# Bilinear field pairs: weight loads in ring order, four-field loads split into single ones, more splits dealt out

## The chip, the cores and the metric

The kernel runs on one core of a Trainium2 chip. The metric is the device time of one execution in microseconds; the time of a kernel is the median of its runs. Five engines share the work: TensorE (PE, with its weight loads as PEld), VectorE (DVE), ScalarE (ACT), GpSimd (POOL) and SyncE (SP), which here only issues transfers. ACT and POOL issue transfers too.

## The reference

There are 32 fields of 128 numbers for each of 1024 rows, and a 128x128 matrix for each of the 496 pairs of fields (i, j) with i < j. Field i goes through the pair's matrix, and the result is multiplied by field j, element by element:

```
v_i = inputs[:, I_IDX, :]
v_j = inputs[:, J_IDX, :]
transformed = jnp.einsum('bpd,ped->bpe', v_i, W)
return transformed * v_j
```

All is float32. The output is 1024 x 496 x 128 numbers, 260 MB, so the stores are by far the largest traffic.

## The kernel before, in words

**Tiling.** Fields lie as 128 x 1024 tiles (embedding on the partitions, rows along the free axis). Pairs are numbered q = 0 to 495 in the order of line 45: i falls from 30 to 0, and j runs upward from i+1. So field i becomes the left operand at q = first_q[i] = (30-i)(31-i)/2, for 31-i pairs. The host lays the weights out as 62 tiles of eight pairs (512 KB each).

**Arithmetic.** The first 15 pairs use plain float32 products (line 227). For the other 481, both operands are split into a high part h and a low part l, and a third part d made from them (names wh, wl, wd and xh, xl, xd). A pair then takes three products for each half of 512 columns: xh·wh and xl·wl (line 230), a scaling of the sum by ACT in place (line 232), and xd·wd added to it (line 241). VectorE multiplies the whole pair, 1024 columns, by field j into an output tile (line 251). An output tile holds four pairs; ACT issues its 2 MB store (line 280).

**Splits.** `split_w` handles two pairs' weights, called a chunk: ACT makes wh (line 137), POOL makes wl and wd (lines 139 to 141). `split_x` handles half a field: ACT makes xh (line 155), POOL makes xl (lines 156 and 157), and VectorE makes xd (line 290) ten half-pair steps later (XDLAG). The list `todo` gives each split the earliest pair at which it may be put into the program. At most one split is taken per pair, the one needed first. A chunk for pair q may be split from pair q-5 on. A field may be split from the start of the field before it, plus one pair (line 174). For fields 1 to 11 (SPREAD = 12, lines 175 and 176) the two halves are dealt out: they come n/5 and 3n/5 pairs after that, where n = 30-i.

**Loads.** SP issues most loads, in program order, and waits at each until its buffer is free. Weight tiles rotate through a ring of three buffers; field 0 (`load_x(0)`) takes one of them once. Weight tiles 12, 14, ... 60 (WAPART) are loaded in two parts, 112 partitions by POOL and 16 by SP (lines 105 and 106), and are put into the program as soon as the tile three places before has been split (lines 286 and 287). The other weight tiles and field 0 have pair numbers worked out ahead (lines 191 to 197): tile c at pair 8c-17, or 8c-11 for tiles 55 and 57; field 0 at 421. Fields 16 to 1 come in four groups of four, each one 2 MB transfer (`load_group`, line 111) at the pairs 52, 141, 219 and 313. For this the host interleaves the four fields of a group, so that a partition's 16 KB lie together.

**Buffers.** There are three output tiles, and each of the four groups' buffers is a further output tile until 20 pairs before its load (`until`, OWAIT). So output tiles fall from seven to three in the course of the run. Four PSUM tiles hold a pair each.

Of the kernel before, what the change touches and what calls it, by code (L numbers as in the profile page):

```python
# [7 lines left out]
F32 = mybir.dt.float32  # L8
# [3 lines left out]
P = 128  # L12
NF = 32
NQ = NF * (NF - 1) // 2
BT = 1024
HB = 512
WC = 2
WL = 8
# [3 lines left out]
SHARED = 26  # L22
XDLAG = 10
LAG = 3
SPREAD = 12
PB = 4
WB = 3
WLEAD = 12
XAFTER = 54
XLEAD = 5  # L30

XG = 4
NE = 14
ROWS = 8 * NE
WAPART = tuple(range(12, 62, 2))
BACK = 3
XAT = (313, 219, 141, 52)
OWAIT = 20
SLAG = 2
PB = 4  # L40

# [7 lines left out]
def kernel(  # L49
# [22 lines left out]
    nc = tc.nc  # L72
# [3 lines left out]
    xpool = ctx.enter_context(tc.tile_pool(name="x", bufs=1))  # L76
# [6 lines left out]
    x_sb = {}  # L83

    def load_x(f, pieces=1, eng=None):
        if f == 0:

            t = rpool.tile([P, WL, P], F32, tag="w", name="x_0").rearrange("p q e -> p (q e)")
        else:
            t = xpool.tile([P, BT], F32, tag=f"x{f}", name=f"x_{f}")  # L90
        s = BT // pieces
        for k in range(pieces):
            (eng or nc.sync).dma_start(out=t[:, k * s : (k + 1) * s], in_=xt[f, :, k * s : (k + 1) * s])  # L93
        x_sb[f] = t

    w_raw = {}
# [3 lines left out]
    def move_on(k):  # L100

        nc.gpsimd.dma_start(out=mark[: 2 * k], in_=xt[0, : 2 * k, :16].rearrange("(b a) n -> a b n", a=k))  # L102

    def load_apart(dst, src):
        nc.gpsimd.dma_start(out=dst[:ROWS], in_=src[:ROWS].rearrange("(b a) m n -> a b m n", a=NE))
        nc.sync.dma_start(out=dst[ROWS:], in_=src[ROWS:])

    def load_group(k):
        t = xpool.tile([P, XG, BT], F32, tag=f"g{k}", name=f"x_g{k}")
        f = XG * k + 1  # L110
        nc.sync.dma_start(out=t, in_=xt[f : f + XG].rearrange("m d b -> (m d b)").rearrange("(d m b) -> d m b", m=XG, b=BT))
        for m in range(XG):
            x_sb[f + m] = t[:, m, :]

    def load_w(c, splits=(0, WL), eng=nc.sync):
        w_raw[c] = rpool.tile([P, WL, P], F32, tag="w", name=f"w_{c}")
        if c in WAPART:
            load_apart(w_raw[c], wt[c])
            return
        for a, b in zip(splits, splits[1:]):  # L120
            eng.dma_start(out=w_raw[c][:, a:b, :], in_=wt[c, :, a:b, :])
# [8 lines left out]
    w_s, spent = {}, []  # L130
# [18 lines left out]
    def split_x(f, a, u):  # L149

        if a == 0:
            x_s[f] = [spool.tile([P, BT], F32R, tag=t, name=f"{t}_{f}") for t in ("xh", "xl", "xd")]
        s = slice(a, a + HB)
        h, l, d = [t[:, s] for t in x_s[f]]
        nc.scalar.mul(h, x_sb[f][:, s], 1.0 - 2.0**-13)  # L155
        nc.gpsimd.tensor_tensor(l, x_sb[f][:, s], h.bitcast(F32), ALU.subtract)  # L156
        nc.gpsimd.tensor_scalar(l, l.bitcast(F32), 1.0 / EPS, 1.0, ALU.mult, ALU.mult)  # L157
        if f > NF - 2 - NATIVE - SHARED:
            later.append((min(u + XDLAG, 2 * first_q[f] + LAG - 1), d, h.bitcast(F32), l.bitcast(F32)))
        else:  # L160
            nc.gpsimd.tensor_tensor(d, h.bitcast(F32), l.bitcast(F32), ALU.subtract)
# [3 lines left out]
    first_q = {i: q for q, (i, j) in reversed(list(enumerate(pairs)))}  # L165
# [6 lines left out]
    for i in range(NF - 2 - NATIVE, -1, -1):  # L172
        for a in range(0, BT, HB):
            at = first_q[i + 1] + 1 if i < NF - 3 - NATIVE else 2
            if 0 < i < SPREAD:
                at += (NF - 2 - i) * (1 + 2 * (a > 0)) // 5
            todo.append((at, first_q[i], lambda u, i=i, a=a: split_x(i, a, u)))
    todo.sort(key=lambda t: t[1])

# [5 lines left out]
    load_w(1, eng=nc.sync)  # L185
    for f in range(NF - 5, NF - 4 - XLEAD, -1):
        load_x(f)
# [3 lines left out]
    w_at = {}  # L191
    for c in range(WB, -(-NQ // WL)):
        free = (c - WB + 1) * WL if (c - WB) * WL < nq0 else 0
        early = 0 if XAFTER < c <= XAFTER + WB else WLEAD - 6
        if c not in WAPART:
            w_at[max(c * WL - 3 * WC - 5 - early, free)] = c
    x_at = XAFTER * WL - 11
    assert x_at not in w_at and len(w_at) == NQ // WL - WB - len(WAPART)

    back = []  # L200
    w_next = list(WAPART)

    ngroup = NF // XG // 2
    group_at = {q: k for k, q in enumerate(XAT)}
    assert all(q < first_q[XG * k + XG + 1] for q, k in group_at.items())
    until = {f"g{k}": q - OWAIT for q, k in group_at.items()}
    used = {t: n - 9 for n, t in enumerate(("s0", "s1", "s2", *sorted(until, reverse=True)))}

    def out_tile(g):
# [9 lines left out]
    def first(u):  # L219
        q, h = divmod(u, 2)  # L220
        i, c = pairs[q][0], q // WC
        r = slice(q % WC * P, (q % WC + 1) * P)
        s = slice(h * HB, (h + 1) * HB)
        if h == 0:
            po[q] = ppool.tile([P, BT], F32, tag="po", name=f"po_{q}")
        if q < nq0:
            nc.tensor.matmul(po[q][:, s], w_raw[q // WL][:, q % WL, :], x_sb[i][:, s], start=True, stop=True)  # L227
        else:
            for t in (0, 1):
                m = nc.tensor.matmul(po[q][:, s], w_s[c][t][:, r], x_s[i][t][:, s], start=t == 0, stop=t == 1)  # L230
                apart(m, scaled.get(u - 1) if h else None)
            scaled[u] = nc.scalar.mul(po[q][:, s], po[q][:, s], 1.0 + EPS)  # L232
            apart(scaled[u], taken.get(q - PB), "TensorE's products, which this waits for, have waited for it")

    def second(u):
        q, h = divmod(u, 2)
        i, j = pairs[q]
        r = slice(q % WC * P, (q % WC + 1) * P)
        s = slice(h * HB, (h + 1) * HB)
        if q >= nq0:  # L240
            m = nc.tensor.matmul(  # L241
                po[q][:, s], w_s[q // WC][2][:, r], x_s[i][2][:, s], start=False, stop=True, skip_group_check=True
            )
            apart(m, scaled[u ^ 1])
        g, k = divmod(q, OG)
        if k == 0 and h == 0:
            ots[g] = out_tile(g)
        if q >= NQ - 2:
            nc.vector.tensor_tensor(ots[g][:, k, s], po[q][:, s], x_sb[j][:, s], ALU.mult)  # L249
        elif h == 1:  # L250
            taken[q] = nc.vector.tensor_tensor(ots[g][:, k, :], po.pop(q), x_sb[j], ALU.mult)  # L251
        if q >= NQ - 2:
            stores.append((u + SLAG, out[g, :, k, s], ots[g][:, k, s]))
        elif g == 0 or q >= NQ - OG:
            if h == 1:
                stores.append((u + SLAG, out[g, :, k], ots[g][:, k]))
        elif k == OG - 1 and h == 1:
            stores.append((u + SLAG, out[g], ots[g]))

    for u in range(2 * NQ + LAG + SLAG):  # L260
        q = u // 2
        if u < 2 * NQ:
            i, j = pairs[q]
            if u % 2 == 0 and j == i + 1 and XG * ngroup < i - 2 - XLEAD:
                load_x(i - 2 - XLEAD)
            first(u)
            if u == 2 * nq0:
                move_on(5)
            if u % 2 == 0 and q in group_at:
                load_group(group_at[q])  # L270
            if u % 2 == 1 and q in w_at:
                load_w(w_at[q])
            if u % 2 == 0 and q in back:
                move_on(16 - NE if w_next else 13)
            if u == 2 * x_at + 1:
                load_x(0)
        if LAG <= u < 2 * NQ + LAG:
            second(u - LAG)
        while stores and stores[0][0] <= u - LAG:
            nc.scalar.dma_start(*stores.pop(0)[1:])  # L280
        if u % 2 == 1:
            ready = [t for t in todo if t[0] <= q]
            if ready:
                ready[0][2](u)
                todo.remove(ready[0])
        if w_next and (XAFTER if w_next[0] == XAFTER + 2 else w_next[0] - WB) in spent:
            load_w(w_next.pop(0))
            back.append(q + BACK)
        while later and later[0][0] <= u:
            nc.vector.tensor_tensor(*later.pop(0)[1:], ALU.subtract)  # L290
    assert not todo and not later and not stores
# [32 lines left out]
```

## Time and profile before

| What | us |
|---|---|
| median of three runs (745.08, 750.95, 749.3) | 749.3 |
| the profiled execution | 751.61 |
| its span, first to last instruction | 749.8 |
| PE busy in the span | 706.0 |
| DVE busy | 641.1 |
| ACT busy | 634.3 |
| POOL busy | 596.2 |

The mean granted clock of TensorE is 0.982. HBM traffic is 49.29 MB read and 260.05 MB written. The span is the time in which instructions ran; the profiled execution's own time is 1.8 us longer. PE busy is no measure of PE at its peak, since the matmuls overlap. A row of the profile's groups gives line, engine, operation, tile written from tile read, shape, count, busy time, mean duration in ns, and then the engine's idle time just before such instructions with what ended it.

### The profile page before, as it was taken

The page shows a single profiled execution, that of the slowest core. Times are in us where ns is not written, and L with a number is a line of the kernel's source. Part 1 is how long each engine was busy: PE and PEld are TensorE (multiplying, and loading weights), DVE is VectorE, ACT ScalarE, POOL GpSimd, SP SyncE. Part 2 cuts the span into 40 slices and gives each one's busy share as a digit, 9 for nine tenths or more (in the row PEclk, how much of TensorE's full clock was granted, in tenths as well). Part 3 has the DMA queues.
Part 4 walks back from the last instruction along what each step waited for, and adds up shares of the span by engine and source line. Part 5 has one row for each costly group of instructions (what it writes and reads, how often), then busy time and mean ns, then how long its engine had stood idle before and what let it go on. Part 6 is the DMA issues. An engine that isn't in the chain of part 4 may idle for free.

```text
span 749.8 us, 10632 instructions
## 1 busy us (share of the span) xinstructions
PE 706.0 (94%) x2946; PEld 554.3 (74%) x2946; DVE 641.1 (85%) x550; ACT 634.3 (85%) x1256; POOL 596.2 (80%) x882
## 2 busy tenths in 40 slices
PE   7999999989999999997999979799999999999894
PEld 3577777777787788885888858688787778777783
DVE  3888999979999999996999959688998888988785
ACT  1298999979999999996999959699899999988893
POOL 1789999988888988986888867768788878887660
PEclk9999999999999999999999989999999999999997
DMA  9999999999999999999999999999999999999988
GB/s 346 421 432 425 427 428 429 423 409 377 407 423 414 422 425 426 424 426 418 426 424 425 424 426 378 420 425 422 412 424 418 420 423 415 409 406 412 422 365 340
DMA packets 32939, 310.04 MB, mean 413 GB/s; under 512 B 5104, under 2 KB 5232, under 8 KB 16752
## 3 DMA queue, kind: packets, MB, share of 16 engines
q10 hardware_dynamic: 19584, 261.10, 83.0%
q1 hardware_dynamic: 8864, 36.77, 12.3%
q0 software_dynamic: 4432, 11.48, 4.1%
q8 instruction: 24, 0.39, 0.2%
q14 instruction: 35, 0.29, 0.1%
HBM read 49.29 MB, written 260.05 MB: 413 GB/s over the span
## 4 chain that ended last, share of the span: by engine, by line
PE 64%; DMA 18%; DVE 10%; issue 3%; ACT 3%; ACTq 0%; POOL 0%; DVEq 0%
PE po L230 40%; PE po L241 20%; DMA out_dram<-ot 17%; DVE ot L251 7%; PE po L227 4%; DVE xd L290 3%; ACT po L232 2%; DMA x<-in_xt_dram 1%; ACT wh L137 0%; DVE ot L249 0%; ACTq L280 0%; POOL wl L139 0%; ACT xh L155 0%; DVEq L251 0%; ACTq L93 0%
## 5 line engine op out<-in xcount | busy, mean ns | idle before, releaser
L232 ACT ACTIVATE po<-po 128x512 f32<-128x512 f32 x962 | 553.1, 584 | 82.7 <-PE po L230 66.4
L251 DVE TENSOR_TENSOR ot<-po,x 128x1024 f32<-128x1024 f32 x358 | 430.8, 1221 | 75.6 <-DMA out_dram<-ot 25.6
L230 PE MATMUL po<-xh,wh 128*128 128x512 f32 x962 | 383.0, 398 | 24.0 <-DVE ot L251 23.0
L241 PE MATMUL po<-xd,wd 128*128 128x512 f32 x962 | 377.9, 393 | 4.8 <-DVE ot L249 2.4
L230 PE MATMUL po<-xl,wl 128*128 128x512 f32 x962 | 378.2, 393 | 3.2 <-POOL wl L139 3.0
L139 POOL TENSOR_TENSOR wl<-w,wh 128x256 fp32r<-128x256 f32 x241 | 186.2, 773 | 74.9 <-ACT wh L137 69.3
L230 PEld LDWEIGHTS po<-xh,wh 128*128 128x128 f32 x962 | 182.2, 189 | 79.6 <-DVE ot L251 42.0
L241 PEld LDWEIGHTS po<-xd,wd 128*128 128x128 f32 x962 | 182.3, 190 | 45.5 <-DVE ot L249 3.2
L230 PEld LDWEIGHTS po<-xl,wl 128*128 128x128 f32 x962 | 182.3, 190 | 41.3 <-POOL wl L139 4.1
L141 POOL TENSOR_TENSOR wd<-wl,wd 128x256 fp32r<-128x256 f32 x241 | 181.1, 751 | 20.1
L251 DVE TENSOR_TENSOR ot<-po,x_g 128x1024 f32<-128x1024 f32 x136 | 165.0, 1223 | 24.2 <-DMA out_dram<-ot 6.7
L140 POOL TENSOR_SCALAR wd<-wh 128x256 fp32r<-128x256 f32 x241 | 100.4, 417 | 20.5
L137 ACT ACTIVATE wh<-w 128x256 fp32r<-128x256 f32 x241 | 98.6, 410 | 7.9 <-DVE ot L251 3.6
L290 DVE TENSOR_TENSOR xd<-xh,xl 128x512 fp32r<-128x512 f32 x52 | 50.6, 974 | 0.3 <-ACT wh L137 0.3
L156 POOL TENSOR_TENSOR xl<-x_g,xh 128x512 fp32r<-128x512 f32 x32 | 41.7, 1304 | 0.5
L157 POOL TENSOR_SCALAR xl<-xl 128x512 fp32r<-128x512 f32 x52 | 36.0, 692 | 4.7
L156 POOL TENSOR_TENSOR xl<-x,xh 128x512 fp32r<-128x512 f32 x20 | 26.3, 1315 | 15.7 <-ACT xh L155 15.5
L227 PE MATMUL po<-x,w 128*128 128x512 f32 x60 | 29.3, 646 | 4.0 <-DMA x<-in_xt_dram 3.9
L227 PEld LDWEIGHTS po<-x,w 128*128 128x128 f32 x60 | 11.9, 205 | 20.6 <-issue 14.4
L155 ACT ACTIVATE xh<-x 128x512 fp32r<-128x512 f32 x20 | 12.3, 624 | 11.4 <-DMA x<-in_xt_dram 11.3
L155 ACT ACTIVATE xh<-x_g 128x512 fp32r<-128x512 f32 x32 | 20.0, 625 | 0.0
L102 POOL DMA_DIRECT2D mark<-in_xt_dram x26 | 16.6, 637 | 0.0
(7 smaller groups left out, 19.9 us busy)
## 6 DMA issues: line engine op xcount, KB each, us to landing
out_dram<-ot ACTq DMA_DIRECT2D x122, 2048.0 KB, 12.6
w<-in_wt_dram SPq DMA_DIRECT2D x36, 512.0 KB, 10.9
w<-in_wt_dram POOLq DMA_DIRECT2D x25, 448.0 KB, 11.6
x_g<-in_xt_dram SPq DMA_DIRECT2D x4, 2048.0 KB, 18.6
x<-in_xt_dram SPq DMA_DIRECT2D x14, 512.0 KB, 9.6
out_dram<-ot ACTq DMA_DIRECT2D x6, 512.0 KB, 8.3
w<-in_wt_dram SPq DMA_DIRECT2D x26, 64.0 KB, 6.4
x<-in_xt_dram ACTq DMA_DIRECT2D x4, 256.0 KB, 5.8
```

The lines of the kernel that those rows point to most:

```text
L137: halved[c] = nc.scalar.mul(h, raw, 1.0 - 2.0**-13)
L139: nc.gpsimd.tensor_tensor(l, raw, h.bitcast(F32), ALU.subtract)
L140: nc.gpsimd.tensor_scalar(d, h.bitcast(F32), EPS, 1.0, ALU.mult, ALU.mult)
L141: nc.gpsimd.tensor_tensor(d, l.bitcast(F32), d.bitcast(F32), ALU.subtract)
L156: nc.gpsimd.tensor_tensor(l, x_sb[f][:, s], h.bitcast(F32), ALU.subtract)
L157: nc.gpsimd.tensor_scalar(l, l.bitcast(F32), 1.0 / EPS, 1.0, ALU.mult, ALU.mult)
L227: nc.tensor.matmul(po[q][:, s], w_raw[q // WL][:, q % WL, :], x_sb[i][:, s], start=True, stop=True)
L230: m = nc.tensor.matmul(po[q][:, s], w_s[c][t][:, r], x_s[i][t][:, s], start=t == 0, stop=t == 1)
L232: scaled[u] = nc.scalar.mul(po[q][:, s], po[q][:, s], 1.0 + EPS)
L241: m = nc.tensor.matmul(po[q][:, s], w_s[q // WC][2][:, r], x_s[i][2][:, s], start=False, stop=True, skip_group_check=True)
L251: taken[q] = nc.vector.tensor_tensor(ots[g][:, k, :], po.pop(q), x_sb[j], ALU.mult)
L290: nc.vector.tensor_tensor(*later.pop(0)[1:], ALU.subtract)
```

## The change: what it does

1. Weight tiles from 12 on, and field 0 among them, are put into the program in one order, `ring`: each as soon as the ring's buffer it takes has been split. For odd tiles this is pair 8c-23 in place of 8c-17. Field 0 stands between tiles 54 and 55, and the tile that takes its buffer is now 57; before it was 58, which stood ahead of 57.
2. A group's four fields are loaded by four transfers of 512 KB each, the highest field first, at the group's pair and 6, 12 and 18 pairs later (XSTEP). They still fill one buffer. The host's interleaving goes.
3. SPREAD goes from 12 to 18, so fields 12 to 17 are dealt out too. The second half now comes 5n/10 pairs after the start in place of 6n/10, for all dealt fields; the first half is as it was.

VectorE's whole-pair multiplication (line 251 before) stands in both kernels alike. The core of the diff:

```
-SPREAD = 12
+SPREAD = 18
+WRING = 12
+XSTEP = 6
...
-    def load_group(k):
-        t = xpool.tile([P, XG, BT], F32, tag=f"g{k}", name=f"x_g{k}")
-        f = XG * k + 1
-        nc.sync.dma_start(out=t, in_=xt[f : f + XG].rearrange("m d b -> (m d b)").rearrange("(d m b) -> d m b", m=XG, b=BT))
-        for m in range(XG):
-            x_sb[f + m] = t[:, m, :]
+    group = {}
+
+    def load_group(k, m):
+        if m == XG - 1:
+            group[k] = xpool.tile([P, XG, BT], F32, tag=f"g{k}", name=f"x_g{k}")
+        f = XG * k + 1 + m
+        x_sb[f] = group[k][:, m, :]
+        nc.sync.dma_start(out=x_sb[f], in_=xt[f])
...
+        if f == 0 and a > 0:
+            spent.append("x")
...
-                at += (NF - 2 - i) * (1 + 2 * (a > 0)) // 5
+                at += (NF - 2 - i) * (2 + 3 * (a > 0)) // 10
...
-        early = 0 if XAFTER < c <= XAFTER + WB else WLEAD - 6
-        if c not in WAPART:
-            w_at[max(c * WL - 3 * WC - 5 - early, free)] = c
-    x_at = XAFTER * WL - 11
+        if c < WRING:
+            w_at[max(c * WL - 3 * WC + 1 - WLEAD, free)] = c
...
-    w_next = list(WAPART)
+    last = NQ // WL
+    ring = [*range(WRING - WB, XAFTER + 1), "x", *range(XAFTER + 1, last)]
...
-    group_at = {q: k for k, q in enumerate(XAT)}
+    group_at = {q + XSTEP * (XG - 1 - m): (k, m) for k, q in enumerate(XAT) for m in range(XG)}
...
-                move_on(16 - NE if w_next else 13)
-            if u == 2 * x_at + 1:
-                load_x(0)
+                move_on(16 - NE if max(w_raw) < WAPART[-1] else 13)
...
-        if w_next and (XAFTER if w_next[0] == XAFTER + 2 else w_next[0] - WB) in spent:
-            load_w(w_next.pop(0))
-            back.append(q + BACK)
+        if ring[WB:] and ring[0] in spent:
+            ring.pop(0)
+            c = ring[WB - 1]
+            if c == "x":
+                load_x(0)
+            else:
+                load_w(c)
+            if c in WAPART:
+                back.append(q + BACK)
...
-    for f in range(1, XG * 4, XG):
-        xt[f : f + XG] = xt[f : f + XG].transpose(1, 0, 2).copy().reshape(XG, P, BT)
```

More of the change, by code (lines that the diff above doesn't have):

```diff
@@ L193 @@
         free = (c - WB + 1) * WL if (c - WB) * WL < nq0 else 0
-        early = 0 if XAFTER < c <= XAFTER + WB else WLEAD - 6
-        if c not in WAPART:
-            w_at[max(c * WL - 3 * WC - 5 - early, free)] = c
-    x_at = XAFTER * WL - 11
-    assert x_at not in w_at and len(w_at) == NQ // WL - WB - len(WAPART)
+        if c < WRING:
+            w_at[max(c * WL - 3 * WC + 1 - WLEAD, free)] = c
     back = []
-    w_next = list(WAPART)
+    last = NQ // WL
+    ring = [*range(WRING - WB, XAFTER + 1), "x", *range(XAFTER + 1, last)]
     ngroup = NF // XG // 2
-    group_at = {q: k for k, q in enumerate(XAT)}
-    assert all(q < first_q[XG * k + XG + 1] for q, k in group_at.items())
-    until = {f"g{k}": q - OWAIT for q, k in group_at.items()}
+    group_at = {q + XSTEP * (XG - 1 - m): (k, m) for k, q in enumerate(XAT) for m in range(XG)}
+    assert all(q + 5 < first_q[XG * k + m + 2] for q, (k, m) in group_at.items())
+    until = {f"g{k}": q - OWAIT for k, q in enumerate(XAT)}
     used = {t: n - 9 for n, t in enumerate(("s0", "s1", "s2", *sorted(until, reverse=True)))}
@@ L269 @@
             if u % 2 == 0 and q in group_at:
-                load_group(group_at[q])
+                load_group(*group_at[q])
             if u % 2 == 1 and q in w_at:
```

## The prediction

> **What bounds the kernel now.** First the page's totals and its slices of the transfers, 18.7 us each.
>
> ```profile
> PE 706.0 (94%) x2946; PEld 554.3 (74%) x2946; DVE 641.1 (85%) x550; ACT 634.3 (85%) x1256; POOL 596.2 (80%) x882
> ...
> GB/s 346 421 432 425 427 428 429 423 409 377 407 423 414 422 425 426 424 426 418 426 424 425 424 426 378 420 425 422 412 424 418 420 423 415 409 406 412 422 365 340
> DMA packets 32939, 310.04 MB, mean 413 GB/s; under 512 B 5104, under 2 KB 5232, under 8 KB 16752
> ```
>
> All engines are busy, but the flattest row is the transfers': 420 to 430 GB/s nearly everywhere. At 427 the 310.04 MB take 726 us, and the span is 749.8. So the end is set by bytes plus the time in which transfers run thin: 24 us. Then the windows by stage (the last three columns are granted clock, DMA share and GB/s):
>
> ```profile
> 56.00:150.00 94.00, 89.94 (x382) 70.64 (x381) 87.92 (x76) 85.75 (x171) 86.70 (x121) 1.00 1.01 427
> 150.00:230.00 80.00, 76.46 (x323) 60.95 (x321) 71.62 (x62) 71.61 (x142) 71.55 (x103) 0.98 0.99 401
> 230.00:450.00 220.00, 209.66 (x899) 170.30 (x899) 191.13 (x165) 195.12 (x389) 184.13 (x276) 0.98 1.01 425
> 450.00:464.00 14.00, 14.00 (x62) 11.54 (x62) 12.91 (x12) 12.63 (x26) 9.89 (x17) 0.99 0.95 368
> 464.00:640.00 176.00, 169.76 (x728) 136.15 (x727) 151.79 (x131) 157.84 (x314) 142.67 (x215) 0.99 1.01 420
> 640.00:700.00 60.00, 58.20 (x249) 46.00 (x248) 51.59 (x45) 53.26 (x106) 47.48 (x74) 1.00 1.00 410
> 700.00:749.80 49.80, 37.17 (x159) 29.43 (x158) 34.81 (x31) 33.04 (x64) 20.98 (x34) 0.91 0.89 369
> ```
>
> Against 427 the losses are 80 x 26/427 = 4.9 us (150 to 230), 1.9 (450 to 464), 2.9 (464 to 640), 2.4 (640 to 700), 6.8 (the tail) and 3.7 in the first 56 us. The change can reach the 4.9 and part of the 2.4.
>
> Why is 150 to 230 thin? The timeline of POOL at field 16's split, with the matmul that PE had waiting there (bracket: idle before, and what ended it):
>
> ```profile
> 152.26 1.31 POOL L156 TENSOR_TENSOR xl<-x_g,xh 128x512 fp32r<-128x512 f32 x1
> 153.66 0.62 POOL L157 TENSOR_SCALAR xl<-xl 128x512 fp32r<-128x512 f32 x1
> 154.36 0.74 POOL L139 TENSOR_TENSOR wl<-w,wh 128x256 fp32r<-128x256 f32 x1
> ...
> 156.77 1.30 POOL L156 TENSOR_TENSOR xl<-x_g,xh 128x512 fp32r<-128x512 f32 x1
> 158.16 0.62 POOL L157 TENSOR_SCALAR xl<-xl 128x512 fp32r<-128x512 f32 x1
> 158.86 1.23 POOL L139 TENSOR_TENSOR wl<-w,wh 128x256 fp32r<-128x256 f32 x1
> ```
> ```profile
> 160.13 0.79 PE L230 MATMUL po<-xl,wl 128*128 128x512 f32 x1 [1.97 <-POOL wl L139]
> ```
>
> Both halves of the field went in with one chunk of weights between them. The next chunk, whose wh ACT had ready at 153.8, came at 158.86, and PE waited. Such double halves come once per field. In the issue and multiply times, four pairs take 5.46 us undisturbed (PE: 24 matmuls at 0.2275 us), but 7.0 us across field 17's split, 9.5 across field 16's, and 6.3 to 6.4 across those of 15 to 12. That is 1.5 + 4.0 + 4 x 0.9 = 9 us of production between 132 and 262 us. A 2 MB store waits 4.2 us in the queue before its first packet at 132 us, but 0.8 to 1.9 us between 165 and 217: the cushion is used up, and DMA runs dry.
>
> SP's own waits, to see whether an earlier place in the program means an earlier load:
>
> ```profile
> SPq L121 <- POOL wl L139: 360.6, 32, 16.4
> SPq L106 <- POOL wl L139: 248.3, 24, 17.3
> ```
>
> It doesn't: SP stands at a load 11 us on average until POOL frees the buffer.
>
> **What the Trainium skill says.** "TensorE: Matmul & The Clock Gate", Part 1: an idle TensorE falls to half rate and needs some 3.4 us of work to come back. Here 1.97 us of idleness sufficed: matmuls step 0.43 us from 160.13 to 163.66, then 0.23, so the stall cost about 2 us more than itself. "SBUF — State Buffer", section on the two separate sides: VectorE and GpSimd exclude each other from a shared port pair. It agrees: xd takes 0.68 us alone and 1.48 at 178.65 beside POOL's work. "DMA: Bandwidth & Descriptors", Queues, rings and completion order: each engine takes turns between queues by the packet. So a 16 KB load packet claims as much of a store's time as the store's own; the stores beside the 2 MB loads indeed took 9.3 to 10.8 us instead of 5.6.
>
> **The change part by part.**
>
> *Splits of 17 to 12 dealt out.* Nothing is added: twelve POOL half-splits of 2.0 us, twelve xh of 0.62, twelve xd of 0.68 to 1.48 move. By the formula, with weight chunks served first, the halves go to pairs 82/86, 94/100, 110/114, 124/130, 140/146 and 158/164, for use at 91, 105, 120, 136, 153 and 171: two or three chunks between them instead of one, and 5 to 7 pairs ahead of use. A chunk costs POOL 2.01 us of the 2.73 that PE takes for it; with issues it catches up about 0.6 per chunk. A double half raises POOL's lag behind ACT by 3.1 to 3.7 us (from 2.4 to 5.5 at field 16, from 0.5 to 4.2 at field 15, start of wl less start of wh); a dealt one by 2.05 + 2.05 - 1.2 to 1.8, so 2.3 to 2.9. Field 17 begins with a lag of 2 and, as halves also start later, I get peaks of about 4.2, against about 4.4 at which PE begins to wait (chunks that came with a lag of 4.2 left PE 0.24 us). The four-us loss and most of the others go. VectorE gets its two xd further apart too. So production gains some 8 us of the 9. The end gains only what DMA gets back: of the 4.9 us I take 4.0 (bounds 0 and 5.5). Beyond 230 the stage is full, so the gain is carried on, as DVE's waits for stores (32.3 us in 25 waits) show.
>
> *The earlier second half for fields 11 to 1.* 2 or 3 pairs earlier; PE is at its pace there, and POOL idles up to 0.6 us per chunk. Nothing; if that cover were gone, one late chunk, 0.9 us per field.
>
> *Ring order.* Odd tiles stand 6 pairs earlier, but SP is already waiting for the buffer; nothing. No load comes later, and without SP's wait it would come at most 6 x 1.365 = 8.2 us earlier. Behind them on SP stand only the next loads. POOL's parts keep their place. Field 0 waits for the same release as before (626.5). Tile 57 takes over tile 58's place at 659 and no longer starts at 663; ACT's wait for it at 675.2 (1.62 us) goes. Tile 58 moves to 663, is needed near 686, and lands in about 11.6. Gain 0.5 (0 to 1.6).
>
> *Single loads.* Four issues of 2 MB become sixteen of 512 KB. 512 packets of 16 KB (median 611 ns in the packet records) become 2048 of 4 KB (159 ns): (2048 x 159 - 512 x 611)/16 = 0.8 us more of all engines' time. SP issues twelve more, at 0.33 to 0.5 us, in its waiting time. Each waits for the eighth transfer before it in SP's and ACT's common program order; that lies 13 to 16 pairs back, 18 to 22 us, against 9 to 20 us that stores and loads take to land. A store on ACT can wait for a single load likewise (for example the one at pair 238 for the load at 225), but SP issues these near pair 213 to 225. Nothing; were one late, ACT's scalings would stand behind the store. At 464 us the 2 MB load had filled the queue; four small ones leave it thinner until about 500: 0.3 us (0 to 1).
>
> Sum: -4.0 - 0.5 + 0.8 + 0.3 = -3.4 us: span 746.4 for 749.8. The profiled execution (751.6) lies 2.3 above the median, so I take the difference to the median: 749.3 - 3.4 = 745.9.
>
> **Rivals.**
> 1. *More is won.* The queue also stays full at 450 to 464 (1.9) and 640 to 700 (another 1.5), and all of 4.9 comes back: 745.9 - 0.9 - 1.9 - 1.5 = 741.6. For: both dips follow stalls. Against: at 438 VectorE waits 6 us as four output tiles become three, which the change leaves as it is.
> 2. *No difference.* POOL is busy without a gap from 56 to 168 us, so it, not the order of its work, may set the pace; then stalls shrink but recur, and 1 us of gain is eaten by the packets: 749.3.
> 3. *Slower.* A second half now stands 5 pairs ahead of use in fields 17 to 15. It takes POOL 2.0 us where a chunk's wl takes 0.74, so PE waits for it when POOL's lag passes about 3.7 us (I expect 2.1; 4.9 to 5.5 was measured at chunks 44 to 52). At a lag of 5, each of six fields costs 1.5 us, plus 2 us of half rate in three of them: 15 instead of 9, with the queue dry, so 749.3 + 6 = 755.
>
> **How the numbers follow.** Forecast 0.52 (743.5 to 748.5), rival 1 0.16, rival 2 0.2, rival 3 0.12. A measurement of this kernel tells about 1% from no change, 7.5 us: below 741.8 is faster, above 756.8 slower. Faster: over half of rival 1 and a little of the forecast's edge, 0.13. Slower: the upper half of rival 3, 0.06. Same: 0.81. The range leaves out the lower end of rival 1 and most of rival 3: 740.5 to 751.5.
>
> **What would show it.** Right: no PE wait for wl over 1 us between 130 and 262; the stage 150 to 230 at 420 GB/s or more; store waits in the queue of 2 us or more at 165 to 217; x_g issues of 512 KB landing in about 10 us; no ACT wait for w near 675. Wrong: PE waiting for xl at the starts of fields 17 to 15; ACT held at a store; GB/s in 230 to 450 below 423.

## The result and the profile after

The changed kernel takes 746.75 us (median of 20 runs, 743.81 to 750.95) against 749.96 us (20 runs of the kernel before beside it, 745.08 to 757.03). The ratio is 0.9966, with a 95% interval of 0.9943 to 0.9988: 2.5 us less, with 0.9 to 4.3 as bounds. (The medians alone differ by 3.2 us; the ratio, which has the interval, is used below.) Some executions of a kernel run over 1.5% longer than its fastest; the ratios leave these out, the medians do not. The profiled execution took 743.81 us (span 742.0) and is the fastest of its twenty, while the one shown of before (751.61) lay above its median. So the two profiles differ by 7.8 us where the kernels differ by some 3. Only what several profiles repeat is given weight below.

First the page's totals, slices of the transfers and packets, after:

```profile
PE 703.8 (95%) x2946; PEld 549.4 (74%) x2946; DVE 636.8 (86%) x550; ACT 634.9 (86%) x1256; POOL 594.8 (80%) x882
...
GB/s 347 427 424 428 427 427 425 430 423 426 427 419 426 423 424 425 425 423 422 425 428 422 428 423 334 420 423 423 423 425 422 426 423 415 430 421 422 424 408 351
DMA packets 34667, 310.04 MB, mean 418 GB/s; under 512 B 5296, under 2 KB 5424, under 8 KB 18992
```

The instructions and bytes are the same; 1728 packets have come in. (Sixteen loads of 512 KB have 1536 packets of data more than four of 2 MB, and each of the twelve added transfers has 16 tiny ones.) The valley of 377 in slices 9 to 11 is gone. A single deep one is left, 334 at 445 to 464 us; it was 378 before. The windows by stage, after (last columns: granted clock, DMA share, GB/s):

```profile
56.00:150.00 94.00, 91.01 (x388) 71.41 (x387) 88.45 (x77) 86.65 (x174) 86.61 (x122) 1.00 1.01 427
150.00:230.00 80.00, 78.76 (x341) 62.99 (x340) 73.76 (x65) 74.73 (x151) 73.73 (x108) 1.00 1.01 424
230.00:450.00 220.00, 208.14 (x882) 165.06 (x881) 185.04 (x162) 192.42 (x381) 180.48 (x271) 0.98 1.00 420
450.00:464.00 14.00, 14.00 (x63) 11.59 (x62) 12.62 (x11) 13.12 (x27) 11.33 (x18) 1.00 0.99 375
464.00:640.00 176.00, 170.55 (x736) 136.59 (x735) 154.10 (x134) 159.59 (x316) 144.57 (x219) 1.00 1.01 423
640.00:700.00 60.00, 59.14 (x256) 47.21 (x255) 52.13 (x45) 54.64 (x109) 47.39 (x74) 1.00 1.01 422
```

150 to 230 us went from 401 to 424 GB/s: 80 x 23/427 = 4.3 us. But 230 to 450 fell from 425 to 420, the sign that the prediction had named as "wrong". It wasn't the loads: cut at 430, the windows give 425 and 424 up to 430, as before, and 374 from 430 to 464, where before had 400. So 34 x 26/427 = 2.1 us were lost there.

Now POOL at field 16's split after the change, and the waits that mattered: PE's for wl before, then two after.

```profile
153.07 1.29 POOL L160 TENSOR_TENSOR xl<-x_g,xh 128x512 fp32r<-128x512 f32 x1
...
155.16 0.74 POOL L143 TENSOR_TENSOR wl<-w,wh 128x256 fp32r<-128x256 f32 x1
...
157.48 0.74 POOL L143 TENSOR_TENSOR wl<-w,wh 128x256 fp32r<-128x256 f32 x1
...
159.50 0.75 POOL L143 TENSOR_TENSOR wl<-w,wh 128x256 fp32r<-128x256 f32 x1
...
161.52 1.29 POOL L160 TENSOR_TENSOR xl<-x_g,xh 128x512 fp32r<-128x512 f32 x1
```
```profile
PE po L230 <- POOL wl L139: 3.0, 2, 2.0
```
```profile
DVE ot L255 <- DMA out_dram<-ot: 33.5, 32, 6.3
...
PE po L234 <- POOL wl L143: 1.0, 2, 0.8
```

Three chunks of weights now stand between the halves where there was one. The waits give total, times and longest: PE's for wl shrank from 3.0 us with a longest of 2.0 (and, in that profile, a half-rate stretch behind it) to 1.0 with 0.8. A 2 MB store issued between 165 and 217 us now waits 3.9 to 4.8 us in the queue before its first packet, where before had 0.8 to 1.9: the queue no longer runs dry there. VectorE's waits for stores rose slightly, from 32.3 us in 25 waits to 33.5 in 32. ACT's wait for a weight tile, 2.2 us before, isn't in the list any more. The multiplication for output tile 41, counted from 0, ended at 254.5 us instead of 262.3.

### The profile page after: what moved, and what is told of

Same layout as the page of the kernel before. It is cut to its first block, busy times and chain, and to the rows that moved or that the text cites. A ratio compares the mean times of both kernels' runs of the same rounds, so it can differ in the third digit from the quotient of the medians.

```text
span 742.0 us, 10650 instructions
## 1 busy us (share of the span) xinstructions
PE 703.8 (95%) x2946; PEld 549.4 (74%) x2946; DVE 636.8 (86%) x550; ACT 634.9 (86%) x1256; POOL 594.8 (80%) x882
## 4 chain that ended last, share of the span: by engine, by line
PE 61%; DMA 23%; DVE 8%; POOL 3%; issue 2%; ACT 1%; DVEq 0%; ACTq 0%; POOLq 0%
PE po L234 38%; DMA out_dram<-ot 23%; PE po L245 19%; DVE ot L255 6%; PE po L231 4%; DVE xd L298 2%; POOL wd L145 1%; POOL wl L143 1%; POOL xl L160 1%; ACT po L236 0%; DMA x<-in_xt_dram 0%; POOL xl L161 0%; POOL wd L144 0%; DVE ot L253 0%; ACT wh L141 0%
## 5 line engine op out<-in xcount | busy, mean ns | idle before, releaser
L144 POOL TENSOR_SCALAR wd<-wh 128x256 fp32r<-128x256 f32 x241 | 101.9, 423 | 20.5
L298 DVE TENSOR_TENSOR xd<-xh,xl 128x512 fp32r<-128x512 f32 x52 | 48.5, 934 | 0.0
L161 POOL TENSOR_SCALAR xl<-xl 128x512 fp32r<-128x512 f32 x52 | 34.4, 662 | 4.6
## 6 DMA issues: line engine op xcount, KB each, us to landing
w<-in_wt_dram POOLq DMA_DIRECT2D x25, 448.0 KB, 11.8
```

Source lines behind the costliest of these rows:

```text
L144: nc.gpsimd.tensor_scalar(d, h.bitcast(F32), EPS, 1.0, ALU.mult, ALU.mult)
```

## The switch from four output tiles to three

The valley left comes where the last group's buffer stops being an output tile. VectorE's timeline after, and PE's:

```profile
441.71 2.36 DVE L255 TENSOR_TENSOR ot<-po,x 128x1024 f32<-128x1024 f32 x2 [6.29 <-DMA out_dram<-ot]
```
```profile
442.99 0.80 PE L234 MATMUL po<-xh,wh 128*128 128x512 f32 x1 [5.43 <-DVE ot L255]
443.58 0.63 PE L234 MATMUL po<-xl,wl 128*128 128x512 f32 x1
444.00 0.63 PE L245 MATMUL po<-xd,wd 128*128 128x512 f32 x1
```

VectorE waits 6.3 us for a store to land, PE stands idle for 5.4 us, and then its matmuls step 0.43 us, half rate, until 448.3. So the next store comes late, and from 446 to 450 the transfers fall to 213 and 123 GB/s. The half rate after idleness is what "TensorE: Matmul & The Clock Gate", Part 1, of the Trainium skill describes; here the granted clock was 0.50 for 6.8 us. The kernel before shows the same wait (6.0 us) and the same half rate, yet its transfers stay at 422 or more from 442 to 450, and then dip to 279 and later 289.

## The experiments

Each ratio is to the kernel before on the same chip. Three chips were used, on which the kernel before has medians of 752.45, 750.23 and 752.21 us. A ratio is not exactly the quotient of two medians.

**The dealing alone.** The kernel before with

```
-SPREAD = 12
+SPREAD = 18
...
-                at += (NF - 2 - i) * (1 + 2 * (a > 0)) // 5
+                at += (NF - 2 - i) * (2 + 3 * (a > 0)) // 10
```

> The kernel before with the splits of fields 17 to 12 dealt out (and the earlier second half), nothing else. Theory A (the gain is DMA time won back between 150 and 230 us, by the dealing): ratio to before 0.993 to 0.996, and the stage 150 to 230 at 420 GB/s or more. Theory B (the gain comes from the single loads, which end the bursts behind which PE stalls and falls to half rate): ratio 0.999 to 1.001, since POOL's total work is the same.

Measured: 747.85 us, ratio 0.9946 (0.9925 to 0.9968). It was run again on the third chip:

> The kernel before with the dealing alone, again, on the same chip as the whole. Both theories: 0.993 to 0.997 (0.9946 before). If it comes out at 0.998 or more, the first result owed something to its chip.

There: 748.39 us, 0.9943 (0.9919 to 0.9967). Its stage, first run:

```profile
150.00:230.00 80.00, 78.91 (x340) 62.97 (x340) 73.73 (x65) 74.70 (x150) 73.73 (x108) 1.00 1.01 424
```

The dealing by itself is worth 4.1 and 4.3 us. It alone fills the valley: the second run has 419 GB/s there.

**The single loads alone.** The kernel before with the diff's lines for `load_group`, XSTEP, `group_at` and the host's order of the fields.

> The kernel before with fields 16 to 1 loaded singly, nothing else. Theory A: no gain, 1.000 to 1.002 (0.8 us more for smaller packets, a thinner queue after 464 us); the stage 150 to 230 stays near 401 GB/s. Theory B: ratio 0.995 to 0.997, with no VectorE wait of over 3 us for a store near 350 and 480 us and the stage 464 to 640 above 420 GB/s.

Measured: 748.7 us, 0.9951 (0.9931 to 0.9971). I had expected a small loss; it is a gain. Run again on the third chip:

> The kernel before with the single loads alone, again. The packets' price of 0.8 us fell with 0.9951; if singles really gain, 0.993 to 0.997 again. If it comes out at 0.999 or more, that result was the chip's, and the packets' price may stand after all.

There: 749.22 us, 0.9968 (0.9945 to 0.9991). The gain, 3.7 and 2.4 us, isn't the chip's. What can be seen of it in the profiles lies after the last group's load; first run:

```profile
464.00:550.00 86.00, 82.38 (x355) 65.54 (x354) 72.94 (x64) 76.99 (x154) 69.53 (x105) 1.00 1.01 424
550.00:640.00 90.00, 88.39 (x381) 70.72 (x381) 80.77 (x70) 82.70 (x165) 74.67 (x113) 1.00 1.01 422
640.00:700.00 60.00, 58.41 (x251) 46.24 (x250) 51.89 (x46) 53.53 (x106) 47.80 (x74) 1.00 1.01 415
```

Before, these three were 421, 419 and 410. That is (86 x 3 + 90 x 3 + 60 x 5)/427 = 1.9 us, and 1.5 us in the second run (423, 422 and 413). The stage 150 to 230 varies by itself, 400 and 410 GB/s, for a reason that is given with the dealing in the section on the prediction.

The other sign that theory B had named came too. These are VectorE's longest waits for a store near 350 and near 480 us, in the kernel before, and then in the first run of the singles:

```profile
349.86 2.36 DVE L251 TENSOR_TENSOR ot<-po,x 128x1024 f32<-128x1024 f32 x2 [4.56 <-DMA out_dram<-ot]
...
483.70 2.35 DVE L251 TENSOR_TENSOR ot<-po,x 128x1024 f32<-128x1024 f32 x2 [4.85 <-DMA out_dram<-ot]
```
```profile
353.00 3.50 DVE L254 TENSOR_TENSOR ot<-po,x_g 128x1024 f32<-128x1024 f32 x3 [1.83 <-DMA out_dram<-ot]
...
488.01 3.52 DVE L254 TENSOR_TENSOR ot<-po,x 128x1024 f32<-128x1024 f32 x3 [1.22 <-DMA out_dram<-ot]
```

Behind the two waits of the kernel before, PE stood idle for 4.5 and 4.0 us, and its clock was halved for 3.4 us each time. All four profiles with 2 MB loads (before, the dealing twice, the ring order) have both waits, of 2.8 to 4.6 us at 337 to 350 and of 3.7 to 4.9 near 480, each with half a clock for 3.4 to 6.8 us. The two of the singles have none of over 2 us there, nor have the three of the changed kernel.

**The ring order alone.** The kernel before with the diff's `ring` and `spent` lines.

> The kernel before with weight tiles and field 0 in ring order, nothing else. Theory A: 0.5 us, ratio 0.998 to 1.000, shown by ACT's wait for tile 57 (1.62 us near 675) going; all other SP loads are issued when POOL frees their buffers, as before. Theory B has nothing to say here: 1.000.

Measured: 750.71 us, 0.9992 (0.9971 to 1.0012). It can be told neither from nothing nor from the half microsecond. The wait of 1.62 us near 675 is gone.

**All but the dealing.** The changed kernel with SPREAD and the formula of before.

> The changed kernel with the dealing undone (fields 1 to 11 only, second half at 6n/10), so ring order and single loads together. Theory A: ratio to before 0.999 to 1.002, PE again waiting for wl for about 2 us near 158. Theory B: 0.996 to 0.998, as the whole change.

Measured: 749.78 us, 0.996 (0.9938 to 0.9982): what the single loads give alone, and PE waits 1.97 us for wl again. The ring order adds nothing to them that could be seen.

**The change again, and its last group earlier.** First the changed kernel on the second chip, as the base there:

> The changed kernel itself once more, beside the experiments on one chip. Dealing alone gave 0.9946, ring order with single loads 0.996. If the parts add up: 0.989 to 0.992. If time won early is given back at the switch from four to three output tiles near 440 us (374 GB/s there in its profile, 423 before): 0.994 to 0.998, as first measured.

Measured: 749.32 us, 0.9971 (0.995 to 0.9992). Beside it, to fill the queue at the switch:

```
-XAT = (313, 219, 141, 52)
+XAT = (293, 219, 141, 52)
...
-    until = {f"g{k}": q - OWAIT for k, q in enumerate(XAT)}
+    until = {f"g{k}": q - OWAIT * (k > 0) for k, q in enumerate(XAT)}
```

> The changed kernel with the last group's four loads from pair 293 on, when its buffer stops being an output tile, in place of pair 313 (the output tiles are used as before). If time is given back at the switch to three output tiles, because VectorE waits there and nothing but stores could fill the queue, the loads now fill it: 430 to 464 us above 400 GB/s and 2 to 4 us less than the changed kernel. If the dip at the switch costs nothing (the queue's total work sets the end and the dip only moves it): no difference from the changed kernel, within 1 us.

Measured: 747.49 us, 0.9943 (0.9922 to 0.9964); 430 to 464 at 386 GB/s against 375 in the base. The first load now went at 435.6 us. The 400 GB/s that the first theory asked for weren't reached, but the time was 2.1 us below the base. That spoke for the switch as the place where gain is lost, but two intervals that overlap don't prove it. A stronger form was run on the third chip, with the group's loads 3 pairs apart, so that two go at 436:

```
-    group_at = {q + XSTEP * (XG - 1 - m): (k, m) for k, q in enumerate(XAT) for m in range(XG)}
+    group_at = {q + (XSTEP if k else 3) * (XG - 1 - m): (k, m) for k, q in enumerate(XAT) for m in range(XG)}
```

> The changed kernel with the last group of four (fields 4 to 1) put 20 pairs earlier, at the moment its output tile is given up, and its four loads 3 pairs apart in place of 6, so that they fill the queue while VectorE waits at the switch from four output tiles to three. Theory A (the dip at the switch, 430 to 464, is where 2 us of the gain goes): the two stages together lose 1 to 2 us less than in the changed kernel, and the ratio is 0.002 to 0.004 below that of the changed kernel on this chip. Theory B (what the switch loses is only moved, since the same buffers are missing): within 0.001 of it.

Measured: 748.61 us, 0.9958 (0.9941 to 0.9974), against the changed kernel's 748.15 and 0.9962 on that chip. Its windows:

```profile
430.00:464.00 34.00, 27.16 (x107) 21.48 (x105) 21.50 (x20) 23.85 (x48) 21.33 (x33) 0.90 1.00 392
464.00:550.00 86.00, 82.73 (x353) 65.37 (x354) 73.62 (x65) 76.10 (x150) 70.06 (x106) 1.00 1.01 420
550.00:640.00 90.00, 86.97 (x375) 69.40 (x375) 77.23 (x67) 81.32 (x162) 72.37 (x110) 1.00 1.00 411
640.00:700.00 60.00, 57.81 (x249) 45.85 (x248) 51.75 (x45) 53.19 (x105) 47.03 (x72) 1.00 1.01 405
```

The switch got back 34 x 17/427 = 1.4 us, as theory A said. But the three stages after it, 424, 421 and 411 in the changed kernel on that chip, ran below that: (86 x 4 + 90 x 10 + 60 x 6)/427 = 3.8 us lost. These are single profiles; the medians, 0.0004 apart, say that nothing is left of the gain. So the numbers of theory B hold for the time.

**More fields dealt out.** The changed kernel with SPREAD = 24, so that fields 18 to 23 are dealt out too.

> The changed kernel with fields 23 to 18 dealt out as well. Between 56 and 150 us the transfers already run at 427 GB/s, so if the end is set by transfers, faster production there only makes the queue longer: no difference from the changed kernel, within 1 us. If production (PE, VectorE, POOL) sets the end, its stalls of 0.5 to 1 us at five field changes go and it is 2 to 4 us faster.

Measured: 750.58 us, 1.000 (0.9975 to 1.0024), where the base on that chip has 0.9971: some 2 us slower, at the edge of the noise, and not faster. PE at one of the new splits (the same comes at 82.93 with 1.32 us), and the stage:

```profile
68.77 0.47 PE L245 MATMUL po<-xd,wd 128*128 128x512 f32 x1 [1.27 <-DVE xd L298]
```
```profile
56.00:150.00 94.00, 87.65 (x377) 69.55 (x376) 84.61 (x75) 83.40 (x168) 85.48 (x119) 1.00 1.01 419
```

In fields of 7 to 12 pairs a dealt second half stands so near its use that its xd, which VectorE makes last, comes too late: PE waits for xd five times, 7.0 us in all, where the first profile of the changed kernel has one wait of 1.2. The stage falls from 427 to 419.

**The four loads together.** The changed kernel with single loads, but all four at the group's pair:

```
-    group_at = {q + XSTEP * (XG - 1 - m): (k, m) for k, q in enumerate(XAT) for m in range(XG)}
+    group_at = {q: k for k, q in enumerate(XAT)}
...
-                load_group(*group_at[q])
+                [load_group(group_at[q], m) for m in range(XG - 1, -1, -1)]
```

> The changed kernel with the four single loads of a group put into the program together, at the group's pair, so only the size of packets and transfers differs from the one 2 MB load. If the single loads gain because they are spread in time: 2 to 4 us slower than the changed kernel, with VectorE waits of 3 us and more for stores near 350 and 480 us. If they gain because 4 KB packets take smaller turns from the stores: as the changed kernel, within 1 us.

Measured: 756.72 us, 1.0066 (1.004 to 1.0091): 0.0095, some 7 us, above the base. SP's issues and ACT's wait:

```profile
215.04 5.55 SPq L117 DMA_DIRECT2D x_g<-in_xt_dram  x4
226.50 0.33 SPq L125 DMA_DIRECT2D w<-in_wt_dram  x1
```
```profile
254.64 0.42 ACT L141 ACTIVATE wh<-w 128x256 fp32r<-128x256 f32 x1 [5.80 <-DMA w<-in_wt_dram]
```

The weight tile that SP issued at 226.50 stood behind the four loads and landed 28.1 us later, where 13.6 is the middle one there. ACT's 5.8 us became 6.4 us of VectorE's waiting for PE (at 257.77). Two such valleys, to 367 and 363 GB/s, can be seen in the slices. So neither theory came out: the kernel is slower, but by weights that come late, and VectorE's waits of over 3 us for a store near 350 and 480 are missing. This run doesn't tell whether the singles gain by their size or by their distance.

**The whole beside its parts.** The changed kernel on the third chip.

> The changed kernel once more, beside the dealing alone and the single loads alone on one chip, to see whether the parts add up. So far: dealing alone 0.9946, singles alone 0.9951 on one chip; all of the change 0.9966 and 0.9971 on two others. Theory A (the parts overlap: either fills the queue, and what the second adds is given back where four output tiles become three): 0.994 to 0.997, not below either part by more than 0.002. Theory B (the parts add, and the chips merely differed): 0.988 to 0.992, clearly below both.

Measured: 748.15 us, 0.9962 (0.9943 to 0.9982), where the dealing has 0.9943 and the singles 0.9968. Theory A's numbers came out: the parts don't add.

## Why the prediction was right, and where it wasn't

It said 745.9, of 749.3: 3.4 us less. It came out 2.5 less by the ratio; the median of 746.75 lies 0.9 above 745.9 and inside the range. The step that carried the forecast, the dealing, was right. The step for the single loads was wrong in sign, and what kept the sum near the truth was luck. By its steps:

*Dealing: -4.0.* Right. The valley was worth 4.3 us by its GB/s (3.7 to 4.3 in three profiles of the changed kernel), and the part alone moved the time by 4.1 and 4.3. But the valley read in the one profile of before was a deep one. Its stall of 1.97 us stands in all five profiles without the dealing (1.97 to 2.02), and half rate followed it in two of them only, before and the first run of the singles, which ran at 401 and 400 GB/s from 150 to 230; the other three kept their clock and ran at 408 to 411. So the 2 us of half rate that the prediction added to the stall came in some executions and not in others. The nine profiles with the dealing ran at 419 to 424. Mean against mean, 406 and 422, that is 80 x 16/427 = 3.0 us; the rest of the 4.1 and 4.3 isn't placed. The cover, too, is thinner than I took it. POOL's lag rose to 5.0 us at field 15, not 4.2; at eight places between 155 and 207 us, PE began 0.05 us after POOL had finished, and it waited up to 0.8 us. So POOL sets the pace there, as rivals 2 and 3 had it, but no longer by microseconds. Production from output tile 19 to 41 sped up by 6.6 us (130.0 to 123.4), not 8.

*Earlier second half for fields 11 to 1: nothing.* It wasn't tried apart from the dealing; 230 to 430 stayed at 425 and 424.

*Ring order: -0.5.* Not refuted, too small to see: 0.9992. The wait of ACT that it was to take away went, with the ring order alone and in the changed kernel.

*Single loads: +0.8 for packets, +0.3 for a thin queue.* Both wrong, in sign. The failed step is "more of all engines' time". I multiplied the packets' durations in the records and charged the sum to the end. With the singles alone the stages with the loads in them, 230 to 330 and 330 to 430, ran at 426 and 425, and at 425 and 425, where before had 425 and 424: no loss. And the queue after 464 wasn't thinner but fuller: the median wait of a store in it, from 464 to 550, was 4.1 and 3.9 us with the singles and 2.7 before.

What I had left out is what the 2 MB load did to VectorE. I had seen that the stores beside it took 9.3 to 10.8 us instead of 5.6, but not followed it on. Counting the packets of the store queue in order, 128 to a store, one store beside each 2 MB load took 8.7 to 11.8 us from first packet to last, in all four profiles with such loads. With single loads at the same pairs none of those beside them took over 8.0. In the kernel before, the two waits of VectorE near 350 and 480 end 0.12 us after just such a store has landed (issued at 328.2 and 467.8, landed at 349.74 and 483.58). Without the stretching the waits are gone. That much is shown. That the 3.7 and 2.4 us come from these waits is likely, but only the 1.9 and 1.5 us above were found in the stages.

Size and distance aren't told apart. With the four loads together the stores beside them took 8.0 us at most as well, so the smaller packets seem enough to end the stretching. That kernel's loss is another one: without the distance, the four loads hold up the weights behind them.

The spread of the engines is no explanation of its own. A transfer counts as landed when its slowest DMA engine is done. From the first to the last of the 16 landing records of a store (median of stores landing at 500 to 550) it was 3.8 us before, 2.8 and 2.7 with the singles and 5.0 with the four together; but the dealing alone, with its 2 MB loads, has 2.4 and 2.9, and the earlier fill has 3.9 though its stage 464 to 550 ran at 425 GB/s.

*x_g landing in about 10 us.* Wrong: 17.0.

```profile
x_g<-in_xt_dram SPq DMA_DIRECT2D x16, 512.0 KB, 17.0
```

A quarter of the 2 MB takes nearly as long as the 2 MB before (18.6). "DMA: Bandwidth & Descriptors", Queues, rings and completion order, says that each engine goes round its queues by the packet. By that, a load in 4 KB packets, beside stores in 16 KB ones, gets a small share in each turn. That a packet of the profile's records is a packet in that page's sense isn't shown here; the times fit it. I had used the rule for the stores but not for the loads. It cost nothing in the changed kernel: no engine waits for an x_g load.

*The sum.* Near the truth because two errors cancel, which is luck. The dealing (-4.1, -4.3) and the singles (-3.7, -2.4) would give some -7 together, and the whole gives 2.2 to 2.9 in three comparisons. About 2 us of the shortfall shows at the switch: 430 to 464 ran at 374, 375 and 375 in three profiles of the changed kernel, at 382 and 385 with the dealing, 391 and 398 with the singles, 400 before. I had taken VectorE's wait there as unchanged, and it was (6.3 for 6.0); what I left out is how deep the queue falls after it. But the kernel with all but the dealing has the deepest valley, 372, and its ratio of 0.996 is still that of the singles. And the two fills show that filling this valley doesn't surely shorten the run. So the switch isn't shown to be the cause. Another difference is on record: near 297 us, where five output tiles become four, VectorE waits 2.6 to 5.1 us for a store in all three profiles of the changed kernel (with half a clock for 6.8 us in two), 2.7 in one of the dealing alone, and not over 2 in those of before and of the singles. But the stage 230 to 330 still ran at 423 to 425 GB/s. What keeps the parts from adding is open.

*Rivals.* The first had 640 to 700 recover: 422 in the first profile, but 416 and 411 in the others, so only in part. The second was right in that POOL's lag recurs, but not in its time. The third didn't come here, but a kin of it shows where fields 18 to 23 are dealt out: there the second half's xd, not its xl, is late. ACT wasn't held at a store: after the first output tile only four were issued more than 0.15 us after their multiplication, the latest 0.6.

## What to carry to other kernels

When bytes set the end, look for stretches where the queue ran dry, and ask what kept production late there; spreading the splits out was worth about what the valley's GB/s said (3.0 to 4.3 us, and 4.1 and 4.3 measured). Don't price packets by their durations in the records when many engines and queues overlap: measure the stage's GB/s. Ask of a large load what it does to the stores beside it, and who waits for them. And try each part alone: here the dealing by itself (0.9946, 0.9943) does as well as the whole (0.9966, 0.9971, 0.9962), and no version tried is clearly faster than the dealing alone.

## What was unexpected of the hardware

- Splitting a 2 MB load into four of 512 KB made the kernel faster (0.9951 and 0.9968), and the same four issued together made it slower than the 2 MB load (1.0066). "DMA: Bandwidth & Descriptors", Rules for kernel authors, asks for at least 1 MiB per DMA for the most bandwidth, and for coalescing small transfers. Beside a queue full of 2 MB stores, the smaller loads did better, as long as no weights stood close behind them.
- Beside a 2 MB load in 16 KB packets a 2 MB store took 8.7 to 11.8 us from first packet to last; beside 512 KB loads in 4 KB packets, at the same places, 8.0 at most.
- A weight tile behind four 512 KB loads on the same queue landed after 28.1 us, with 13.6 as the usual time beside it.
- The sixteen engines that share a transfer end apart: in the kernel before by 1.8 us (median of stores landing at 150 to 200) to 4.9 (at 400 to 442), and by 6.4 at most.
- The same stall of PE, about 2.0 us at the same place of the program, was followed by half a clock for 3.4 us in two profiles and by none in three.
